# A gated MLP with ternary down projection on one core: down_w's loads and roundings, the first batch's order, and VectorE's planned work in slots 7 and 8

## The chip, the core and the metric

The kernel runs on one core of a Trainium2 chip. The time is the device time of one execution in microseconds (us); runs of the kernel before gave 723.7, 724.06 and 725.07, so its median is 724.06. One more execution was profiled. The engines of the core work on their own instruction queues: PE (TensorE, matrix products), DVE (VectorE), ACT (ScalarE), POOL (GpSimd), and SP (SyncE), which here only issues DMA transfers. Each engine takes its instructions in program order, and an instruction that waits holds back all behind it on its engine.

## What is computed

```python
scale = cond @ norm_w.T + 1.0
ms = jnp.mean(x * x, axis=-1, keepdims=True)
h = x * (scale[:, None, :] * jax.lax.rsqrt(ms + EPS))
u = h @ up_w.T
val, gate = jnp.split(u, 2, axis=-1)
h = val * jax.nn.gelu(gate, approximate=False)
y = act_quant(h) @ weight_quant(down_w).T        # forward value
return y + x
```

`act_quant` scales each token by 127 over its largest magnitude, rounds, clips and scales back; `weight_quant` makes down_w ternary (-1, 0, 1) with one scale, the mean of its magnitudes. x is 4 x 1024 x 512, up_w 4096 x 512 (2048 rows of value, 2048 of gate), down_w 512 x 2048, all in float32.

## The kernel before, in words

**Batches and slots.** The four batches of x are worked off one after the other, each in 16 slots. A slot makes 128 of the 2048 hidden features for the batch's 1024 tokens (two halves of 512). Precision comes from splitting each float32 operand into a high and a low float16 part (`s_high`, `s_low` and their likes make them, in ACT and in DVE or POOL).

**The product.** From slot 13 of batch 1 on, a slot is a Strassen-like form with 7 products, each of six matmuls (class `Slot`, `product` at L690), on sums of weight blocks and sums of token blocks. The products go to PSUM banks A, E and B: `first` (A), which ACT copies to B (`first_copy`, L797), `fourth` (E), `second` (on to B), `third` (A), `fifth` (A), `gate` (E) and `value` (A). DVE and ACT close the slot: `third_out` (L825) and `value_out` (L845) on DVE write the hidden activations H, `gate_sum` (L833) on DVE frees the E bank, and two Gelus run on ACT. Slots 0 to 12 of batch 1 are done without it: each half has a gate and a value of 12 matmuls (`half_gate`, `half_gelu`, `half_value`, `half_out`, L705 to L761), because the sums of weights are not there yet.

**The weights.** In batch 1 each slot's weight rows are loaded (`w_load`), scaled by a power of two (`w_range`, `w_factor`, `w_scale`), split (`w_rows_high`, `w_rows_low`), turned by a transposing DMA (`w_rows_turn`), and then summed for the 7-product form: `s_sum` (L429) makes four sums of a slot in float32, `s_high` (L446) and `s_low` (L450) split them. Both `s_sum` and `s_low` run on POOL, or on DVE where the step's name ends in a further `.1`. For slots 13 to 15 the split sums stand in rows (`s_rows`, two buffers of the tag `xr`) and are turned by `s_turn` (L468). All sums are stored in HBM by `s_spill` (L462), and each later batch loads them back, slot by slot, two slots ahead: `s_load` (L478, L476) with four parts named `s_load.g.n`, where slot g counts on from 16 for batch 2. They go to the double buffer SXY.

**down_w.** Its eight parts of 512 KB are fetched a second time by `d_fetch(n)` (L539), rounded by `d_round` (L543) and made ternary by `d_sign` (L550), both on ACT, the latter into a buffer of the tag `xr`, and turned pairwise by `d_turn` (L553) into `wd`. The buffers of the fetches are borrowed from the tokens. Parts 0 to 5 are fetched in the first batch; `D_MOVES` has the fetches and turns that follow in slots of batch 2, and `D_LATE` the roundings and signs, with their slot and their place in it (x, y or z).

**Down projection.** That of a batch runs in slots 10 to 13 of the next one, which makes those slots longer (15.2 us against 9.07).

**What sets the order.** For the first batch an order written out by hand: the string `FIRST_BATCH` (L1355) holds 609 steps such as `s_low.15.0` (name, slot, part) and `slot.15.1` (slot, index in `SLOT_STEPS`: 0 `first`, 1 `first_copy`, 2 `fourth`, 7 `second_gelu`, 11 `gate_sum` and so on), and `take` (L1350) issues them one by one. This gives the program order of every engine, SP included. It ends with the transfers for slots 0 and 1 of batch 2 (`s_load.16.n`, `s_load.17.n`). `t_turn.3` (L665), the turn of the last tokens of batch 2, stands among the steps before them.

For batches 2 to 4 a planner (`Filler`, L1441) places the rest of DVE's and ACT's work, above all the largest magnitude of each token (`pair_max`, L886 to L898). Each item has a cost in us and a slot from which it may run. Each slot has a budget:

```python
left = SLOT_US + PAIR_US * down - OWN_US + 0.4
more = D_SUM_US * len(late_sums) + 0.7 * (j + 1 == min(DOWN) and b + 1 < B)
left -= D_SUM_US * len(early_sums) + more
```

(L1574 to L1576; SLOT_US is 9.07). `run(p)` (L1581) then spends it at the places x and z of the slot, and what does not fit waits for the next one.

Of the kernel before, what the change touches and what calls it, by code (L numbers as in the profile page):

```python
# [51 lines left out]
def glu_quant_kernel(  # L52
# [1297 lines left out]
    def take(steps):  # L1350
# [5 lines left out]
        w_load.3 d_load.6 d_load.3 t_load.0 d_load.5 d_load.4 s_sum.0.1 o_whole.2.2.0 gate.1.0 w_range.3  # L1356
        x_scale.6 w_factor.3 gelu.1.0 turn.4 s_sum.0.0.1 turn.5 w_load.4 x_scale.7 s_sum.0.2 w_range.2
        turn.6 turn.7 w_load.5 o_whole.0.0.0 x_high.0 value.1.0 x_high.3 x_low.0 d_load.2 d_load.7 x_high.1
        x_low.3 x_high.2 w_factor.2 s_high.0.0 x_low.1 d_sum.4 x_low.2 gate.0.1 o_whole.1.0.1 out.1.0
        w_scale.2.1 w_scale.2.0 value.0.1 s_sum.0.3.1 rows_high.2 s_high.0.1 rows_low.2 rows_turn.2  # L1360
        w_scale.3.1 w_scale.3.0 o_WHOLE.3.2.1 gelu.0.1 gate.1.1 rows_high.3 s_low.0.0.1 d_sum.5 w_load.9
        s_sum.1.0.1 s_sum.1.2.1 w_range.4 rows_low.3 value.1.1 s_low.0.1.1 s_spill.0.0 gelu.1.1 s_sum.1.3.1
        t_square.0.0 out.1.1 d_load.0 s_high.1.1 gate.2.0 w_range.5 c_largest w_factor.4 d_sum.6 s_sum.1.1.1
        w_load.10 o_sum.0 s_high.1.0 rows_turn.3 value.2.0 out.0.1 w_scale.4.1 d_sum.7 s_low.1.0 w_scale.4.0
        c_over w_factor.5 gate.2.1 s_sum.2.0 rows_high.4 o_sum.1 w_scale.5.0 s_low.1.1 s_spill.1.0 c_range
# [5 lines left out]
        c_spread s_spill.2.2 c_rows gate.4.0 out.3.0 t_square.0.1 w_scale.6.1 s_sum.3.2 max.0.0.0 d_sum.1
        s_sum.3.3 max.1.0.0 o_high.0 s_sum.3.1 w_load.8 value.4.0 t_root.0 w_scale.6.0 max.1.0.1 rows_high.6
        out.3.1 s_high.3.0 o_low.0 gate.4.1 w_range.7 rows_low.6 rows_turn.6 gelu.4.0 w_factor.7 s_high.3.1
        w_scale.7.1 s_low.3.1.1 value.4.1 s_low.3.0.1 s_sum.4.1 w_scale.7.0 gelu.4.1 s_sum.4.0 s_spill.3.0
        c_undo rows_high.7 t_load.1 c_copy d_total out.4.0 gate.5.0 w_range.8 rows_low.7 rows_turn.7 out.4.1
        s_sum.4.2.1 s_sum.4.3 value.5.0 s_high.4.0 w_factor.8 c_store w_gain.6 s_low.4.0.1 w_scale.8.1
        s_spill.5.1 s_spill.6.1 gelu.5.0 s_sum.5.0.1 c_load s_sum.5.1 out.5.0 w_scale.8.0 d_spread gate.5.1
        rows_high.8 max.0.1.0 rows_low.8 value.5.1 rows_turn.8 gelu.5.1 s_sum.5.2.1 w_range.9 s_high.4.1
        s_low.4.1 w_factor.9 gate.6.0 max.1.1.0 w_scale.9.0 s_sum.5.3 s_high.5.0 d_mean gelu.6.0 max.1.1.1
        s_spill.3.2 s_low.5.0.1 s_spill.4.0 value.6.0 s_spill.7.1 c_bring w_scale.9.1 s_spill.5.0 out.5.1  # L1380
        w_gain.8 t_scale.0.1 s_high.5.1 s_low.5.1 rows_high.9 s_sum.6.0.1 gate.6.1 s_spill.8.1 s_sum.6.1.1
        t_scale.0.0 s_sum.6.2.1 t_high.0.0 rows_low.9 s_high.6.0 value.6.1 rows_turn.9 t_high.0.1
        t_sum.0.0.1 w_range.10 t_low.0.0 t_sum.0.1.1 t_sum.0.2.1 gelu.6.1 w_factor.10 w_scale.10.1
        t_sum.0.3.1 gate.7.0 s_low.6.0.1 t_high.0.2 out.6.0 s_sum.7.0 w_scale.10.0 s_sum.6.3.1 s_spill.4.2
        t_low.0.2 s_high.6.1 s_spill.5.2 value.7.0 rows_high.10 s_low.6.1.1 w_gain.10 t_low.0.1 t_turn.0
        t_square.1.1 out.6.1 t_square.1.0 s_sum.7.1.1 s_sum.7.2.1 gate.7.1 t_root.1 s_sum.7.3.1 w_range.11
        t_scale.1.1 s_high.7.0 w_factor.11 w_scale.11.0 s_low.7.0.1 value.7.1 gelu.7.0 s_spill.6.0
        rows_low.10 rows_turn.10 s_high.7.1 s_low.7.1 gelu.7.1 out.7.0 w_scale.11.1 gate.8.0 s_sum.8.0.1
        s_sum.8.1.1 s_sum.8.2.1 s_high.8.0 out.7.1 s_spill.7.0 s_sum.8.3.1 s_high.8.1 value.8.0 s_low.8.0.1
        s_spill.8.0 gelu.8.0 s_sum.9.0.1 s_low.8.1.1 s_spill.8.2 s_sum.9.1.1 s_sum.9.2.1 s_high.9.0  # L1390
        s_low.9.0 t_scale.1.0 gate.8.1 s_sum.9.3.1 w_load.12 rows_high.11 max.2.0.0 s_spill.6.2 w_range.12
        rows_low.11 value.8.1 rows_turn.11 max.2.0.1 t_sum.1.0.1 out.8.0 t_sum.1.2 max.3.0.0 gate.9.0
        gelu.8.1 t_sum.1.3 max.3.0.1 w_factor.12 w_scale.12.0 s_spill.9.1 out.8.1 t_load.2 value.9.0
        s_spill.11.1 t_high.1.1 t_sum.1.1.1 s_high.9.1 s_low.9.1 s_sum.10.1.1 gelu.9.0 max.2.1.0 t_high.1.2
        s_sum.10.0 max.2.1.1 w_scale.12.1 gate.9.1 s_sum.10.2 max.3.1.0 s_spill.9.2 rows_high.12 s_spill.7.2
        s_spill.9.0 s_sum.10.3.1 s_high.10.1 max.3.1.1 w_load.13 value.9.1 rows_low.12 rows_turn.12
        t_low.1.2 out.9.0 s_high.10.0 gate.10.0 gelu.9.1 t_high.1.0 t_square.2.1 t_low.1.0 w_range.13
        t_low.1.1 t_turn.1 value.10.0 out.9.1 s_low.10.0.1 gelu.10.0 t_square.2.0 s_low.10.1.1 s_sum.11.0.1
        t_root.2 s_sum.11.2.1 gate.10.1 w_factor.13 s_sum.11.3 s_sum.11.1.1 s_high.11.1 t_scale.2.1
        w_load.14 s_high.11.0 t_load.3 t_scale.2.0 value.10.1 w_scale.13.0 t_sum.2.0.1 w_scale.13.1 out.10.0  # L1400
        rows_high.13 s_low.11.0.1 s_spill.11.0 w_range.14 s_sum.12.0.1 gate.11.0 s_sum.12.1.1 s_spill.10.1
        s_sum.12.2.1 s_spill.10.2 s_low.11.1.1 s_spill.12.1 t_sum.2.2.1 t_sum.2.1.1 s_spill.10.0 rows_low.13
        rows_turn.13 s_high.12.0 value.11.0 t_sum.2.3.1 t_high.2.1 w_factor.14 w_gain.12 t_high.2.2
        s_low.12.0.1 t_low.2.2 t_high.2.0 gelu.10.1 gate.11.1 out.10.1 gelu.11.1 s_spill.12.0 t_low.2.1
        t_low.2.0 t_turn.2 s_sum.13.1.1 value.11.1 s_sum.12.3.1 s_sum.13.0.1 s_sum.13.2.1 gelu.11.0 out.11.1
        s_high.12.1 t_square.3.0 s_high.13.0 gate.12.0 t_square.3.1 w_scale.14.0 s_low.13.0.1 s_sum.14.0
        out.11.0 w_load.15 s_turn.13.0 value.12.0 s_low.12.1.1 gelu.12.0 t_root.3 s_sum.13.3.1 s_spill.13.0
        s_high.13.1 w_scale.14.1 s_low.13.1.1 rows_high.14 s_sum.14.2 s_turn.13.1 gate.12.1 out.12.0
        s_sum.14.3 s_spill.13.2 w_range.15 rows_low.14 rows_turn.14 t_scale.3.1 value.12.1 s_high.14.0
        s_low.14.0 s_sum.14.1.1 t_sum.3.0.1 w_factor.15 w_scale.15.0 s_turn.14.0 w_scale.15.1 slot.13.0  # L1410
# [404 lines left out]
```

## Time and profile before

| what | value |
|---|---|
| median of the runs | 724.06 us (723.7 to 725.07) |
| the profiled execution | 723.61 us, of which the span of the trace is 721.8 us |
| PE | busy 714.7 us, 99% of the span |
| DVE | 589.7 us, 82% |
| ACT | 422.0 us, 58% |
| POOL | 126.0 us, 17% |
| mean granted clock of PE | 0.999 |
| HBM | 53.50 MB read, 23.09 MB written |

The trace has a start and a duration for every instruction. A row of a timeline reads: start in us from the span's beginning, duration, engine, line of the kernel, operation, output <- inputs, and in square brackets how long the engine stood idle before and what it waited for. PEld is the loading of weights into the array, which runs beside the products; SPq are the DMA issues on SP's queue. A chain of waits goes back from the end of the program, at each step to what released the work; "issue" is time in which an engine waited for nothing that the trace shows.

### The profile page before, as it was taken

How to read it: one execution, taken by the hardware profiler on the slowest of the kernel's cores; microseconds unless marked ns; L12 is line 12 of the kernel's file. 1: busy time of each engine (PE TensorE's matmuls, PEld its weight loads, DVE VectorE, ACT ScalarE, POOL GpSimd, SP SyncE). 2: the span in 40 equal slices, each digit the busy share in tenths (PEclk: the TensorE clock that was granted, in tenths of full speed). 3: DMA queues.
4: the chain of work that ended last, by engine and by line, in shares of the span. 5: the costliest groups of instructions: out<-in, count | busy, mean ns of one | idle time of the engine just before them, and what ended most of it. 6: DMA issues, size and time to landing. Idle time of an engine off the chain costs nothing.

```text
span 721.8 us, 10211 instructions
## 1 busy us (share of the span) xinstructions
PE 714.7 (99%) x3670; PEld 360.1 (50%) x3670; DVE 589.7 (82%) x889; ACT 422.0 (58%) x700; POOL 126.0 (17%) x132
## 2 busy tenths in 40 slices
PE   8999999999999999999999999999999999999998
PEld 4544444444444446665444445665444444445854
DVE  8898998877898899887789887676688888755896
ACT  6998875776667774554335676544433665333473
POOL 1532222140100124340100030460020000000120
PEclk9999999999999999999999999999999999999999
DMA  7799987999995665777845646765944545442253
GB/s 277 259 280 288 245 200 231 281 219 258 278 189 117 132 160 146 192 185 165 172 102 101 129 101 188 178 166 162 212 103 103 102 102 103 101 102 90 103 175 117
DMA packets 230003, 123.01 MB, mean 170 GB/s; under 512 B 191401, under 2 KB 201277, under 8 KB 229954
## 3 DMA queue, kind: packets, MB, share of 16 engines
q1 hardware_dynamic: 229802, 122.24, 68.3%
q8 instruction: 28, 0.46, 0.3%
q14 instruction: 21, 0.17, 0.1%
q10 hardware_dynamic: 152, 0.13, 0.1%
HBM read 53.50 MB, written 23.09 MB: 106 GB/s over the span
## 4 chain that ended last, share of the span: by engine, by line
PE 95%; DMA 1%; ACT 1%; DVE 1%; SPq 1%; issue 1%; DVEq 0%; ACTq 0%
PE A L690 35%; PE E L690 17%; PE po L1052 9%; PE pg L705 9%; PE pv L705 9%; PE B L690 9%; PE po_end L1004 4%; DMA SXY<-s_dram 1%; PE pz L1169 1%; DMA s_dram<-s_rows 1%; PE ptx L1153 1%; PE pv L776 0%; PE po_B L1052 0%; PE pg L776 0%; PE pw L375 0%
## 5 line engine op out<-in xcount | busy, mean ns | idle before, releaser
L690 PEld LDWEIGHTS <-SXY 128*128 128x128 f16 x2100 | 205.4, 98 | 242.2 <-issue 1.3
L690 PE MATMUL A<-R,SXY 128*128 128x512 f16 x1164 | 269.0, 379 | 0.5 <-DMA SXY<-s_dram 0.5
L690 PE MATMUL E<-R,SXY 128*128 128x512 f16 x588 | 142.9, 379 | 0.1
L825 DVE SCALAR_TENSOR_TENSOR H<-A,sg,t 128x512 f32<-128x512 f32 x51 | 38.3, 750 | 71.0 <-PE A L690 70.9
L976 DVE TENSOR_TENSOR H<-H,am 128x1024 f32<-128x1024 f32 x64 | 76.1, 1215 | 0.0
L836 ACT ACTIVATE t<-t,sg 128x512 f32<-128x512 f32 x51 | 36.8, 721 | 65.7 <-DVE t L833 65.6
L690 PE MATMUL B<-R,SXY 128*128 128x512 f16 x300 | 72.9, 379 | 0.3 <-ACT B L797 0.3
L896 DVE TENSOR_REDUCE gm<-H 128x512 f32<-128x1024 f32 x56 | 69.0, 1232 | 1.1
L705 PEld LDWEIGHTS <-SXY 128*128 128x128 f16 x390 | 38.1, 98 | 45.9 <-DVE SXY L417 0.4
L819 ACT ACTIVATE t<-B,sg 128x512 f32<-128x512 f32 x51 | 35.0, 687 | 35.6 <-PE B L690 35.5
L912 POOL PARTITION_ALL_REDUCE am<-R x8 | 14.3, 1793 | 233.2 <-DVE R L898 233.2
L1052 PE MATMUL po<-wd,R 128*128 128x256 fp8e4 x416 | 52.4, 273 | 0.0
L812 ACT COPY t<-A 128x512 f32<-128x512 f32 x51 | 29.6, 580 | 36.1 <-PE A L690 35.8
L805 ACT COPY v<-E 128x512 f32<-128x512 f32 x51 | 29.9, 585 | 32.3 <-PE E L690 27.3
L1052 PEld LDWEIGHTS <-R 128*128 128x128 bf16 (+1 forms) x448 | 43.8, 98 | 8.9
L705 PE MATMUL pg<-R,SXY 128*128 128x512 f16 x204 | 46.8, 379 | 0.0
L797 ACT COPY B<-A 128x512 f32<-128x512 f32 x51 | 29.2, 572 | 29.9 <-PE A L690 29.2
L845 DVE SCALAR_TENSOR_TENSOR H<-v,sg,t 128x512 f32<-128x512 f32 x51 | 40.1, 786 | 6.4 <-ACT t L836 6.3
L705 PE MATMUL pv<-R,SXY 128*128 128x512 f16 x186 | 43.4, 379 | 0.0
L984 ACT ACTIVATE H<-H 128x1024 f32<-128x1024 f32 x38 | 39.9, 1050 | 5.2 <-DVE H L976 5.2
L842 DVE TENSOR_TENSOR v<-A,v 128x512 f32<-128x512 f32 x51 | 34.9, 684 | 8.8 <-PE A L690 7.6
L898 DVE TENSOR_TENSOR R<-R,gm 128x512 f32<-128x512 f32 x56 | 40.9, 730 | 1.1
(236 smaller groups left out, 926.2 us busy)
## 6 DMA issues: line engine op xcount, KB each, us to landing
SXY<-s_dram SPq DMA_DIRECT2D x48, 256.0 KB, 2.9
H<-in_L_cond_up_w_dram SPq DMA_DIRECT2D x13, 512.0 KB, 4.1
s_dram<-SXY SPq DMA_DIRECT2D x16, 384.0 KB, 3.6
SXY<-s_dram SPq DMA_DIRECT2D x48, 128.0 KB, 3.1
xr<-in_x_dram SPq DMA_DIRECT2D x19, 256.0 KB, 3.1
out_dram<-xr SPq DMA_DIRECT2D x19, 256.0 KB, 2.5
H<-in_x_dram SPq DMA_DIRECT2D x8, 512.0 KB, 7.7
R<-in_L_cond_down_w_dram SPq DMA_DIRECT2D x8, 512.0 KB, 6.9
```

What stands on the lines that cost most here:

```text
L690: PE.matmul(o, s[:, w, k, :], operand(g // NJ, c, l, k), start=start and n == 0, stop=stop and n == len(TERMS) - 1, skip_group_check=True,)
L705: PE.matmul(ps, a[k // 2][:, w, k % 2, :], XP[:, l, k, h * TOK : (h + 1) * TOK], start=n == 0, stop=n == len(terms) - 1,)
L819: ACT.activation(self.t1, self.B, AF.Gelu, scale=gain(self.g, 1))
L825: DVE.scalar_tensor_tensor(h_half(self.g, 0), self.A, gain(self.g, 0), self.t1, ALU.mult, ALU.mult)
L836: ACT.activation(self.t2, self.t2, AF.Gelu, scale=gain(self.g, 1))
L842: DVE.tensor_tensor(self.v, self.A, self.v, ALU.add)
L845: DVE.scalar_tensor_tensor(h_half(self.g, 1), self.v, gain(self.g, 0), self.t2, ALU.mult, ALU.mult)
L896: DVE.tensor_reduce(gm[0], v, AX.X, ALU.max, apply_absolute_value=True)
L898: return [largest, lambda: DVE.tensor_tensor(m, m, gm[0], ALU.max)]
L976: DVE.tensor_tensor(v, v, r.to_broadcast([P, 2, TOK]), ALU.mult)
L984: ACT.activation(v, v, AF.Copy, bias=MAGIC)
L1052: PE.matmul(po, w[:, j], m, start=start and j == 0, stop=stop and j == n - 1, skip_group_check=True,)
```

## The change

It has three parts. (1) `KEPT_US` takes 3.0 us off the planner's budget in slots 7 and 8, in every batch but the last. (2) The fetches of down_w's parts 4 and 5 leave the first batch for slots 0 and 1 of batch 2, the turns 2 and 3 of down_w stand in slots 3 and 4, and parts 4 to 7 are rounded and signed a slot later. (3) `FIRST_BATCH` is written in a new order. PE's instructions stay in the old order. 14 steps of sums and differences go from POOL to DVE (among them `s_sum.2.0`, `s_sum.14.0`, `s_sum.15.1`, `s_sum.15.3`, `t_sum.3.2`) and 14 from DVE to POOL (among them `s_sum.0.0`, `s_low.12.1`, `s_sum.15.0`, `t_sum.3.1`, `s_low.15.0`); SP has two steps less. Of the string only the lines around slot 4 and the end are shown.

```diff
     D_LATE = [
         ((0, "x"), d_round, 2), ((0, "x"), d_sign, 2), ((0, "y"), d_round, 3),
-        ((1, "x"), d_sign, 3), ((1, "x"), d_round, 4), ((1, "y"), d_sign, 4),
-        ((2, "x"), d_round, 5), ((2, "x"), d_sign, 5), ((2, "y"), d_round, 6),
-        ((3, "x"), d_sign, 6), ((3, "x"), d_round, 7), ((3, "y"), d_sign, 7),
+        ((1, "x"), d_sign, 3), ((2, "x"), d_round, 4), ((2, "x"), d_sign, 4),
+        ((2, "y"), d_round, 5), ((3, "x"), d_sign, 5), ((3, "x"), d_round, 6),
+        ((3, "y"), d_sign, 6), ((4, "x"), d_round, 7), ((4, "x"), d_sign, 7),
     ]
     D_MOVES = {
-        0: ((d_turn, 0),),
-        1: ((d_turn, 1), (d_fetch, 6)),
-        2: ((d_turn, 2), (d_fetch, 7)),
+        0: ((d_turn, 0), (d_fetch, 4)),
+        1: ((d_turn, 1), (d_fetch, 5), (d_fetch, 6)),
+        2: ((d_fetch, 7),),
+        3: ((d_turn, 2),),
         4: ((d_turn, 3),),
     }
...
     FIRST_BATCH = """
...
-        rows_turn.4 o_high.3 s_sum.2.2.1 gate.3.0 s_sum.2.3.1 out.2.0 s_high.2.1 rows_high.5 s_low.2.1
-        o_sum.2 d_sum.2 value.3.0 w_gain.4 o_sum.3 d_sum.3 o_high.2 o_low.1 w_load.6 gelu.2.1 rows_low.5
...
+        gate.3.0 s_sum.2.0.1 rows_high.5 s_sum.2.2.1 s_sum.2.3.1 o_low.1 o_high.2 s_high.2.1 rows_low.5
+        value.3.0 d_sum.2 s_spill.2.1 w_load.6 o_sum.3 w_load.11 d_sum.3 w_gain.4 s_low.2.1.1 gelu.2.1
...
-        rows_turn.15 t_high.3.0 slot.13.6 gains s_low.14.1.1 slot.13.5 t_high.3.2 t_low.3.0 slot.13.13
-        s_sum.15.1 gelu.12.1 s_turn.14.1 s_sum.15.3 s_high.15.0 slot.14.0 out.12.1 t_high.3.1 slot.13.3
-        s_spill.14.2 t_low.3.2 d_fetch.1 slot.13.7 slot.14.2 slot.14.1 slot.13.14 s_high.15.1 s_low.15.1
-        s_spill.13.1 t_low.3.1 slot.14.6 s_low.15.0.1 s_turn.15.0 slot.13.8 s_spill.15.0 d_round.0 t_turn.3
-        slot.14.4 slot.13.9 max.4.0.0 slot.13.10 slot.14.5 slot.14.3 max.4.0.1 slot.14.13 slot.13.11
-        max.5.0.0 slot.13.12 slot.15.0 d_sign.0 s_turn.15.1 slot.13.15 max.5.0.1 slot.14.7 slot.15.2
-        s_load.16.0 slot.15.1 s_spill.15.1 max.4.1.0 s_load.16.1 d_round.1 slot.15.6 slot.14.14 slot.15.3
-        max.4.1.1 d_fetch.2 slot.14.8 slot.15.7 s_spill.15.2 max.5.1.0 slot.15.4 slot.15.5 slot.14.9
-        slot.14.10 d_sign.1 slot.15.13 s_load.17.1 slot.14.11 slot.15.14 slot.14.12 max.5.1.1 max.6.0.0
-        d_fetch.3 s_spill.11.2 s_load.16.3 slot.14.15 max.6.0.1 s_load.17.0 s_load.16.2 max.6.1.0
-        s_spill.12.2 d_fetch.5 max.6.1.1 s_spill.14.1 d_fetch.4
...
+        t_sum.3.1 t_sum.3.2.1 slot.13.4 t_high.3.0 s_spill.13.1 gelu.12.1 out.12.1 s_spill.14.0 slot.13.6
+        slot.13.5 t_high.3.1 t_sum.3.3.1 slot.13.3 t_low.3.0 slot.13.13 t_high.3.2 rows_low.15 rows_turn.15
+        slot.13.7 t_low.3.2 slot.14.0 slot.14.1 t_low.3.1 slot.14.2 slot.13.14 s_spill.14.2 gains
+        s_sum.15.2.1 s_high.15.0 s_low.15.0 d_fetch.1 max.4.0.0 slot.14.6 s_turn.15.0 w_gain.15 slot.13.8
+        slot.13.9 slot.14.7 slot.14.4 s_spill.15.0 s_sum.15.3.1 s_high.15.1 s_low.15.1 t_turn.3 slot.13.10
+        slot.14.5 slot.14.3 slot.14.13 d_round.0 slot.13.11 max.4.0.1 d_sign.0 slot.15.0 max.5.0.0 slot.15.1
+        slot.15.2 s_turn.15.1 max.5.0.1 d_round.1 slot.14.14 s_load.16.0 slot.15.6 max.4.1.0 s_load.16.1
+        d_sign.1 slot.14.8 max.4.1.1 slot.13.12 d_fetch.2 max.5.1.0 s_spill.15.1 d_fetch.3 slot.15.4
+        s_spill.15.2 slot.13.15 slot.14.9 slot.14.10 slot.15.5 slot.15.3 slot.15.7 slot.15.13 slot.14.11
+        slot.15.14 slot.14.12 slot.14.15 max.5.1.1 s_load.17.0 max.6.0.0 s_spill.14.1 s_load.17.1 max.6.0.1
+        s_spill.12.2 max.6.1.0 s_load.16.3 max.6.1.1 s_spill.11.2 s_load.16.2
     """
...
     OWN_US = 3.0
+    KEPT_US = {7: 3.0, 8: 3.0}
...
             left -= D_SUM_US * len(early_sums) + more
+            if b + 1 < B:
+                left -= KEPT_US.get(j, 0)
```

More of the change, by code (lines that the diff above doesn't have):

```diff
@@ L1355, in glu_quant_kernel @@
     FIRST_BATCH = """
[L1356 to L1365, printed above, removed]
@@ L1371, in glu_quant_kernel @@
[L1371 to L1380, printed above, removed]
@@ L1381, in glu_quant_kernel @@
[L1381 to L1410, printed above, removed]
@@ new lines, in glu_quant_kernel @@
+        out.2.1 gate.3.1 s_high.2.0 gelu.3.0 o_low.3 w_load.7 d_sum.0 o_low.2 value.3.1 w_range.6
+        s_spill.3.1 s_spill.4.1 s_low.2.0.1 s_sum.3.0 rows_turn.5 gelu.3.1 w_factor.6 t_square.0.1 out.3.0
+        c_spread w_scale.6.0 c_rows gate.4.0 s_spill.2.2 s_sum.3.1 max.0.0.0 w_scale.6.1 s_spill.2.0 d_sum.1
+        s_sum.3.2.1 max.1.0.0 s_sum.3.3 rows_high.6 t_root.0 value.4.0 o_high.0 rows_low.6 rows_turn.6
+        w_range.7 out.3.1 o_low.0 gate.4.1 s_high.3.0 w_factor.7 w_load.8 t_load.1 gelu.4.0 s_low.3.0.1
@@ new lines, in glu_quant_kernel @@
+        t_sum.0.2.1 w_factor.10 w_scale.10.1 t_sum.0.3 s_low.6.0.1 s_sum.7.0 gate.7.0 w_gain.10 t_high.0.2
+        out.6.0 s_sum.6.3.1 w_scale.10.0 t_low.0.2 s_high.6.1 rows_high.10 value.7.0 out.6.1 t_square.1.0
+        s_low.6.1.1 t_low.0.1 t_turn.0 t_square.1.1 s_sum.7.1.1 s_sum.7.2.1 t_root.1 t_scale.1.1 gate.7.1
+        w_range.11 s_sum.7.3.1 s_high.7.0 w_factor.11 gelu.7.0 s_low.7.0.1 value.7.1 s_high.7.1 gelu.7.1
+        rows_low.10 s_spill.7.0 w_scale.11.0 s_spill.5.2 out.7.0 s_spill.6.0 s_spill.6.2 s_low.7.1.1
@@ new lines, in glu_quant_kernel @@
+        gate.8.0 rows_turn.10 s_sum.8.0.1 s_sum.8.1.1 s_sum.8.2.1 s_high.8.0 out.7.1 s_sum.8.3.1
+        w_scale.11.1 s_low.8.0.1 s_spill.8.0 s_high.8.1 value.8.0 gelu.8.0 s_sum.9.0.1 s_low.8.1.1
+        rows_high.11 s_sum.9.1.1 s_sum.9.2.1 s_high.9.0 s_low.9.0 t_scale.1.0 s_sum.9.3.1 w_load.12 gate.8.1
+        w_range.12 max.2.0.0 t_load.2 rows_low.11 value.8.1 rows_turn.11 max.2.0.1 t_sum.1.0.1 out.8.0
+        t_sum.1.2 max.3.0.0 gelu.8.1 gate.9.0 t_sum.1.3 t_high.1.1 max.3.0.1 w_factor.12 w_scale.12.0
@@ new lines, in glu_quant_kernel @@
+        t_sum.1.1.1 s_spill.8.2 out.8.1 s_high.9.1 s_low.9.1 s_spill.9.1 value.9.0 t_high.1.2 max.2.1.0
+        s_spill.11.1 s_sum.10.1 w_scale.12.1 max.2.1.1 rows_high.12 s_sum.10.0.1 max.3.1.0 gate.9.1
+        s_sum.10.2 t_high.1.0 s_spill.7.2 s_spill.9.0 s_sum.10.3.1 t_low.1.2 w_load.13 s_spill.9.2
+        rows_low.12 value.9.1 rows_turn.12 gelu.9.1 gelu.9.0 max.3.1.1 t_square.2.1 out.9.0 s_high.10.0
+        t_low.1.1 gate.10.0 gelu.10.0 out.9.1 t_low.1.0 s_low.10.0.1 t_turn.1 s_sum.11.0.1 value.10.0
@@ new lines, in glu_quant_kernel @@
+        s_sum.11.2.1 t_square.2.0 s_high.10.1 s_low.10.1.1 t_root.2 w_range.13 gate.10.1 t_scale.2.1
+        s_sum.11.3 w_factor.13 s_sum.11.1 s_high.11.0 w_load.14 t_sum.2.0.1 out.10.0 t_load.3 value.10.1
+        w_scale.13.0 t_scale.2.0 s_high.11.1 t_sum.2.1.1 w_scale.13.1 t_sum.2.2.1 gelu.10.1 s_low.11.0.1
+        s_spill.11.0 rows_high.13 gate.11.0 s_low.11.1.1 t_sum.2.3.1 w_range.14 s_spill.10.1 s_sum.12.0.1
+        s_spill.12.1 s_sum.12.1.1 s_sum.12.2.1 s_spill.10.0 s_high.12.0 rows_low.13 value.11.0 t_high.2.2
@@ new lines, in glu_quant_kernel @@
+        w_factor.14 s_low.12.0.1 s_spill.12.0 w_scale.14.0 t_low.2.2 t_high.2.0 rows_turn.13 w_scale.14.1
+        gate.11.1 out.10.1 t_high.2.1 t_square.3.1 s_sum.13.0.1 t_square.3.0 t_low.2.0 t_low.2.1 t_turn.2
+        w_gain.12 t_root.3 gelu.11.1 value.11.1 out.11.1 s_sum.12.3 gelu.11.0 s_sum.13.1 s_high.12.1
+        rows_high.14 s_sum.13.2 s_low.12.1 s_high.13.0 gate.12.0 gelu.12.0 s_sum.13.3.1 t_scale.3.1
+        w_load.15 out.11.0 s_low.13.0.1 s_turn.13.0 value.12.0 t_sum.3.0.1 s_high.13.1 s_sum.14.0.1
@@ new lines, in glu_quant_kernel @@
+        rows_low.14 s_spill.13.0 s_low.13.1.1 s_turn.13.1 w_range.15 gate.12.1 w_gain.14 w_factor.15
+        s_spill.10.2 s_sum.14.1.1 w_scale.15.1 s_spill.13.2 w_scale.15.0 value.12.1 t_scale.3.0 rows_turn.14
+        out.12.0 d_fetch.0 slot.13.0 s_sum.14.2.1 s_high.14.0 s_low.14.0 s_sum.14.3.1 s_high.14.1
+        s_low.14.1.1 s_turn.14.0 s_sum.15.0 s_sum.15.1.1 slot.13.2 slot.13.1 s_turn.14.1 rows_high.15
+        t_sum.3.1 t_sum.3.2.1 slot.13.4 t_high.3.0 s_spill.13.1 gelu.12.1 out.12.1 s_spill.14.0 slot.13.6
```

26 lines of the change are left out of this document (21 added, 5 removed).

## The prediction

> **What bounds the kernel.** I read the page first: its span, the line of PE, and the shares of the chain that ended last.
>
> ```profile
> span 721.8 us, 10211 instructions
> PE 714.7 (99%) x3670; PEld 360.1 (50%) x3670; DVE 589.7 (82%) x889; ACT 422.0 (58%) x700; POOL 126.0 (17%) x132
> PE 95%; DMA 1%; ACT 1%; DVE 1%; SPq 1%; issue 1%; DVEq 0%; ACTq 0%
> ```
>
> PE is busy 99% of the span and 95% of the chain is PE. The diff leaves PE's instructions and their order alone. What it can win is therefore time in which PE stood still, and what it can lose is new standing still. So the second view is the busy time by windows of 20 us (the first number after the width is PE's).
>
> ```profile
> 160.00:180.00 20.00, 19.66 (x92) 8.80 (x90) 14.94 (x21) 12.35 (x19) 1.54 (x2) 1.00 1.04 252
> 180.00:200.00 20.00, 19.50 (x91) 8.73 (x90) 17.22 (x23) 13.04 (x18) 3.59 (x2) 1.00 1.09 275
> 260.00:280.00 20.00, 19.96 (x109) 10.47 (x108) 19.17 (x24) 12.54 (x21) 1.80 (x2) 1.00 0.60 159
> ```
>
> Two windows around the end of the first batch, the seam, lose 0.34 and 0.50; around 262 PE loses 0.04, and once more around 432. The granted clock is 1.00 in all of them. The timeline of PE shows the seam's two waits with their releasers, and the chain shows the other two.
>
> ```profile
> 170.04 1.46 PE L690 MATMUL E<-wd,SXY 128*128 128x512 f16 x6
> 171.83 1.45 PE L690 MATMUL B<-R,SXY 128*128 128x512 f16 x6 [0.34 <-ACT B L797]
> ...
> 188.03 1.47 PE L690 MATMUL A<-R,SXY 128*128 128x512 f16 x6 [0.50 <-DMA SXY<-s_dram]
> ```
>
> ```profile
> 259.43 2.59 PE A L690 x12
> 262.02 0.04 issue
> 262.06 1.46 PE E L690 x6
> ```
>
> ```profile
> 431.71 0.04 issue
> 431.74 1.46 PE E L690 x6
> ```
>
> Twelve matmuls take 2.59 in the chain, so a product of six starts 1.30 us after the one before it. The one at 171.83 came 1.79 after 170.04: 0.49 lost. That is 0.15 more than the idle time in its bracket, because the chain counts 1.46 for the first six after a wait, 0.16 over 1.30. In the same way the one at 188.03 lost 0.50 + 0.16 = 0.66, and those at 262.02 and 431.71 lost 0.04 + 0.16 = 0.20 each. The four sum to 1.55 us.
>
> **The ceiling.** The profiled execution took 723.61 (1.81 outside the span); the median shown is 724.06, 0.45 higher. Without the four waits it is 722.06, or 722.5 on the median's footing: 0.22%. A measurement of this kernel tells about 0.2% from no change, which is 1.45 us. Even a change that does all it can is barely visible. There is no such ceiling on a loss.
>
> **Part 1: VectorE queues less in slots 7 and 8 (KEPT_US).** At 262 the fourth product of slot 9 needs the E bank that `gate_sum` of slot 8 (L833) frees. The timeline of DVE:
>
> ```profile
> 247.81 0.75 DVE L825 SCALAR_TENSOR_TENSOR H<-A,sg,t 128x512 f32<-128x512 f32 x1 [1.31 <-PE A L690]
> ...
> 254.37 1.21 DVE L898 TENSOR_TENSOR R<-R,gm 128x512 f32<-128x512 f32 x1
> 255.62 1.25 DVE L896 TENSOR_REDUCE gm<-H 128x512 f32<-128x1024 f32 x1
> 256.90 0.69 DVE L898 TENSOR_TENSOR R<-R,gm 128x512 f32<-128x512 f32 x1
> 257.51 0.74 DVE L825 SCALAR_TENSOR_TENSOR H<-A,sg,t 128x512 f32<-128x512 f32 x1
> ...
> 261.32 0.68 DVE L833 TENSOR_TENSOR t<-E,t 128x512 f32<-128x512 f32 x1
> ```
>
> `gate_sum` ends at 262.00 and PE starts at 262.06. Between 254.37 and 257.51 DVE worked off three steps of the planned maxima, and `third_out` (257.51) queued behind them. One slot earlier it started as soon as PE released it, and a slot is seven products, 9.07 us: 247.81 + 9.07 = 256.88, so it was 0.63 late, and the three steps behind it kept that delay up to `gate_sum`. Worked through the planner, 3.0 us less in slot 7 takes all three steps of its z place out (3.15 us, 254.37 to 257.51) and one of the three in its x place. `gate_sum` then ends near 261.4, and PE needs it 0.20 before 262.06, near 261.8: the wait goes with 0.4 to spare. The same items lie in the same slots of batch 3 at 431. **−0.20 and −0.20.**
>
> What is put off must fit later. The planner moves some 3.9 us of batch 2's maxima to the end of slot 12, executed as slot 13 begins. Slots 12 and 13 of batch 2 are these windows (third number: DVE):
>
> ```profile
> 300.50:315.70 15.20, 15.20 (x100) 9.58 (x98) 14.96 (x20) 6.90 (x14) 9.04 (x11) 1.00 0.67 159
> 315.70:330.90 15.20, 15.20 (x100) 9.60 (x98) 12.03 (x18) 6.19 (x11) 3.18 (x4) 1.00 0.60 162
> ```
>
> Slot 13 would have 12.03 + 3.9 = 15.9 in 15.2, so 0.7 runs over into slot 14, but slot 12 ran at 14.96 and PE lost nothing in it. I take 0; if the overrun falls on the next `gate_sum`, it costs at most that 0.7.
>
> **Part 2: two loads and four roundings of down_w.** Two loads of 512 KB leave the seam's queue, one for each of the first two slots of batch 2. The windows above give DMA shares of 1.04 and 1.09 there: it is full, so leaving it helps whatever stands behind. The transfers of 155 to 195 have the row
>
> ```profile
> dn<-in_L_cond_down_w_dram SPq DMA_DIRECT2D x5, 512.0 KB, 5.5
> ```
>
> (median us from issue to landing). Parts 4 and 5 are rounded in slot 2, at least a slot of 9.07 after their new issue, so 5.5 is covered; a load that came later than that would hold ACT's queue by the difference. The roundings (ACT) come a slot later; ACT had 12.35 and 13.04 of 20, so I take 0, and up to 0.2 against it, the size of one slot-9 wait.
>
> **Part 3: the order of the first batch.** At the seam the chain of waits leads to two transfers:
>
> ```profile
> 164.43 4.92 DMA s_dram<-s_rows
> ...
> 182.63 5.35 DMA SXY<-s_dram
> ```
>
> and SP, which issues the transfers in order, has
>
> ```profile
> 162.92 1.45 SPq L468 DMA_TRANSPOSE SXY<-s_rows  x1
> 165.80 5.24 SPq L665 DMA_TRANSPOSE R<-nx  x1
> ...
> 182.63 1.95 SPq L478 DMA_DIRECT2D SXY<-s_dram  x2
> ```
>
> *The wait at 188* is `s_load.17.0`, landing 5.35 after its issue at 182.63, behind `s_load.17.1`, `d_fetch.3`, `s_spill.11.2` and `s_load.16.3`. In the new order it stands ahead of `s_load.17.1`, `s_load.16.3` and `s_spill.11.2`. It still has to wait until `s_spill.15.1` has landed. I put its issue at 181.5 to 182 and, since the rest of the queue is shorter, its landing at 185 to 187, against a need at 187.3. **−0.66**; if it lands no earlier, 0.
>
> *The wait at 171.8* is the copy of slot 15's first product (L797), two steps behind `d_sign.0` (L550), which waits until `s_spill.15.0` has landed and its buffer is free (164.43 + 4.92). That pair stays, and the landing decides. Two changes push it. `s_low.15.0` goes from DVE to POOL:
>
> ```profile
> L450 DVE TENSOR_TENSOR s_rows<-H,s_rows x4: 683/684/693, 143.8 to 162.2; 128x512 f16<-128x512 f32 x4
> L450 POOL TENSOR_TENSOR s_rows<-H,s_rows x2: 1159/1440/1720, 151.6 to 164.9; 128x512 f16<-128x512 f32 x2
> ```
>
> so 0.48 to 1.04 more; and `s_high.15.0`, which feeds it, now stands behind a copy of slot 14 on ACT and behind the landing of `s_spill.14.0`. Together I estimate 0.9 to 2.7 us for `s_turn.15.0` (162.92) and all that SP has behind it. For it: `d_sign.0` no longer has the Gelu of slot 14 between itself and the copy (0.67), and one load less competes. So the wait lies between gone (−0.49) and 1.4 (+0.9); I take **0**, the row as it stands.
>
> *Elsewhere in the batch* 14 sums and differences go from POOL to DVE and 14 the other way, so the load of neither changes much; I added up the work ahead of each step in the old and the new order, and it shifts by less than 1 us. The tightest place that I found is the E bank of slot 4's value, on DVE and on PE:
>
> ```profile
> 61.40 0.73 DVE L761 SCALAR_TENSOR_TENSOR H<-g,sg,pv 128x512 f32<-128x512 f32 x1
> ```
>
> ```profile
> 62.41 1.46 PE L705 MATMUL pv<-R,SXY 128*128 128x512 f16 x6
> ```
>
> The bank is free at 62.13, 0.28 ahead of its use, and the step's weights (`w_load.6`) now stand behind one more spill (`s_spill.2.1`, 128 KB). I estimate the shift at 0.2 to 0.5, which makes 0 to 0.2. With a second such place I take **0**, and up to +0.5.
>
> One rule speaks against this part. The Trainium skill, "SBUF — State Buffer", section "Who interferes with whom", says that a VectorE instruction with two SBUF inputs and a GpSimd instruction that reads SBUF exclude each other for a whole instruction. The trace agrees: in the two rows below a VectorE operation on two columns ends at 43.43, just as the GpSimd one does at 43.42. By that rule `s_low.15.0` would take the upper 1.72 whenever DVE holds such an operation, which belongs to rival B.
>
> ```profile
> 42.07 1.36 DVE L325 TENSOR_TENSOR undo<-wam,undo 128x2 int32<-128x2 int32 x1
> 41.77 1.65 POOL L450 TENSOR_TENSOR SXY<-H,SXY 128x768 f16<-128x768 f32 x1 [10.91 <-ACT SXY L446]
> ```
>
> **The sum.** −0.40 (slot 9, twice) − 0.66 (188) + 0 (171.8) + 0 (the rest) = −1.06. From 723.61 that is 722.55 for a profiled execution, and **723.0** on the median's footing: −0.15%, within what is told from no change.
>
> **The rivals.**
> A. *All four waits go.* The landing of `s_spill.15.0` comes by 169.4 and nothing else appears: −1.55, 722.5. For it: the Gelu taken out ahead of the copy and the freed queue. Against it: everything ahead of that spill comes later.
> B. *SP is late at the seam: slower.* `s_low.15.0` on POOL holds `s_turn.15.0`, and behind that `t_turn.3` (5.24 on SP), the spill and all loads of slots 16 and 17. At 2.7 late the wait at 171.8 is 1.4 (+0.9); `s_load.17.0` wins some 1.7 of issue time by its new place and loses 2.7, so the wait at 188 is 0.66 + 1.0. With −0.40 for slot 9: 723.61 + 0.9 + 1.0 − 0.40 = 725.1, on the median's footing 725.5 or 725.6. It is visible as slower from about 3.0 us of waits at the seam (1.15 now, 0.40 won back, 1.45 for the bound), which is about 2.7 us of delay. Against it: the transpose has room. Its kind lands in 4.4 by the row below, so 162.92 + 1.45 + 4.4 = 168.8 against the fourth product of slot 15 at 170.04, and a delay under 1.2 costs nothing there.
>
> ```profile
> SXY<-s_rows SPq DMA_TRANSPOSE x2, 4.4
> ```
>
> C. *The seam stays as it is*, or one wait is traded for another of its size: −0.40 alone, 723.66.
>
> **Chances and range.** Forecast 0.36, A 0.22, B 0.28, C 0.14. A, at 0.22%, counts as faster; B as slower; the others as the same: 0.22, 0.50, 0.28. The lower end is A less 0.36, by which the fastest run shown (723.7) lies below its median: 722.2 rounded up. The upper end takes in B's price, 725.5; beyond it I leave some 0.15 of B's chance. The likeliest case's own range, with the unknowns of part 3, is 722.5 to 723.9.
>
> **What would show it.** After the change PE's windows of 260 and 420 should read 20.00; if 19.96 is still there, the planner's step failed. The product that starts at 188.03 should follow without idle time, and `s_load.17.0` should be issued before 182.63. The timeline of SP should show `s_turn.15.0` between 163.8 and 165.6; earlier than that, A, and later, B. New waits at other lines in PE's list of waits, above all below 160 us or around 331, would make the prediction wrong.

## The result and the profile after

Over 22 runs each, the median went from 724.41 to 722.98 us: a ratio of 0.998 with a 95% interval of 0.9973 to 0.9988, or 0.9 to 2.0 us less. The interval does not reach 1: the gain is small, but clear of the scatter. The forecast was 723.0 against 724.06. The profiled execution after the change took 722.53 (span 720.7), that of before 723.61.

The page of the changed kernel, its span, the line of PE and the shares of the chain:

```profile
span 720.7 us, 10220 instructions
PE 714.1 (99%) x3670; PEld 359.9 (50%) x3670; DVE 591.9 (82%) x889; ACT 422.1 (59%) x700; POOL 123.0 (17%) x132
PE 95%; DMA 2%; DVE 1%; ACT 1%; issue 0%; DVEq 0%
```

The share of PE is the same, so it says nothing; the windows do (the first number after the width is PE's).

```profile
160.00:180.00 20.00, 20.00 (x95) 9.00 (x94) 15.32 (x23) 12.24 (x19) 2.69 (x3) 1.00 1.04 234
180.00:200.00 20.00, 19.55 (x90) 8.49 (x89) 17.25 (x24) 11.01 (x15) 3.59 (x2) 1.00 0.93 240
200.00:220.00 20.00, 19.57 (x92) 8.71 (x91) 17.38 (x21) 13.40 (x18) 0.00 (x0) 1.00 1.08 212
260.00:280.00 20.00, 20.00 (x111) 10.59 (x109) 18.72 (x24) 13.33 (x24) 1.94 (x2) 1.00 0.59 159
420.00:440.00 20.00, 20.00 (x95) 9.02 (x93) 13.11 (x18) 15.16 (x22) 5.51 (x6) 1.00 0.56 145
```

The losses at 171.8, 262 and 432 are gone. At 180 to 200 there is still one of 0.45, and a new one of 0.43 at 200 to 220. PE's timeline of the changed kernel shows that these are other waits than before:

```profile
183.65 1.46 PE L690 MATMUL E<-R,SXY 128*128 128x512 f16 x6
185.16 2.75 PE L690 MATMUL A<-R,SXY 128*128 128x512 f16 x12
188.24 1.47 PE L690 MATMUL E<-R,SXY 128*128 128x512 f16 x6 [0.33 <-DVE H L845]
...
194.73 2.75 PE L690 MATMUL A<-R,SXY 128*128 128x512 f16 x12
197.54 1.47 PE L690 MATMUL E<-R,SXY 128*128 128x512 f16 x6
...
204.03 2.75 PE L690 MATMUL A<-R,SXY 128*128 128x512 f16 x12
207.21 1.47 PE L690 MATMUL E<-R,SXY 128*128 128x512 f16 x6 [0.43 <-DMA SXY<-s_dram]
```

A group of six should follow after 1.30, one of twelve after 2.59. So 185.16 is 0.21 late, 188.24 is 0.49 late, 197.54 is 0.22 late and 207.21 is 0.59 late: 1.5 us in all, where the seam cost 1.15 before. From here on the size of a wait is counted in this way, as time lost, unless it is called idle time or stands in a row's bracket. The one at 185.16 waits for a copy on ACT, which stands behind a ternary step of down_w that waits for a spill:

```profile
183.49 1.15 ACT L550 ACTIVATE tn<-H,unmagic 128x1024 fp8e4<-128x1024 f32 x1 [0.45 <-DMA s_dram<-s_rows]
184.54 0.57 ACT L812 COPY t<-A 128x512 f32<-128x512 f32 x1
```

The last three are the fourth products of slots 17, 18 and 19, whose weights come by DMA. The row at 188.24 names DVE's `value_out` (L845), but that step does not touch the E bank; `gate_sum` of slot 15, which frees it, had ended at 186.66. The weight loads beside it name the true releaser:

```profile
PEld L690 <- DMA SXY<-s_dram: 2.3, 3, 0.9
```

Three waits, 2.3 us of idle time on PEld. A row of PE can name an engine that only happened to finish last; the rows of PEld read nothing but the weights.

**The two profiles, product by product.** All 3670 matmuls can be compared by their starts. From before to after the difference changes at these places only: −0.64 in the first 8 us, −0.49 at 171, +0.22 at 185, −0.66 at 188 (first product of slot 17), +0.48 at 188 (its fourth), +0.24 at 197, +0.60 at 207, −0.19 at 262, −0.20 at 432, and −0.44 behind the last product. They sum to the 1.1 us between the spans. The start scatters in both orders (`h2_spill_first`, below, has the new order and the long start of the kernel before). Without it and the end, PE's own waits balance to 0.0. So the two profiles alone do not explain what 44 runs measured, and the experiments had to.

### The profile page after: what moved, and what is told of

The parts are those of the page before. It is cut to its first block, busy times and chain, and to the rows that moved or that the text cites. A ratio compares the mean times of both kernels' runs of the same rounds, so it can differ in the third digit from the quotient of the medians.

```text
span 720.7 us, 10220 instructions
## 1 busy us (share of the span) xinstructions
PE 714.1 (99%) x3670; PEld 359.9 (50%) x3670; DVE 591.9 (82%) x889; ACT 422.1 (59%) x700; POOL 123.0 (17%) x132
## 4 chain that ended last, share of the span: by engine, by line
PE 95%; DMA 2%; DVE 1%; ACT 1%; issue 0%; DVEq 0%
PE A L690 34%; PE E L690 18%; PE po L1052 9%; PE pg L705 9%; PE pv L705 9%; PE B L690 9%; PE po_end L1004 4%; DMA SXY<-s_dram 2%; PE pz L1169 1%; PE ptx L1153 1%; DVE gm L896 1%; PE pv L776 0%; PE po_B L1052 0%; PE pg L776 0%; DVE R L898 0%; PE pw L375 0%
## 5 line engine op out<-in xcount | busy, mean ns | idle before, releaser
L845 DVE SCALAR_TENSOR_TENSOR H<-v,sg,t 128x512 f32<-128x512 f32 x51 | 40.1, 786 | 6.6 <-ACT t L836 6.5
```

Of the source, the lines that this page charges most:

```text
L845: DVE.scalar_tensor_tensor(h_half(self.g, 1), self.v, gain(self.g, 0), self.t2, ALU.mult, ALU.mult)
```

## The experiments

**The parts one by one, and the kernel before once more.** `e1_kept` is the kernel before with

```diff
+    KEPT_US = {7: 3.0, 8: 3.0}
...
+            if b + 1 < B:
+                left -= KEPT_US.get(j, 0)
```

> The kernel before with KEPT_US alone. Theory 1 (each part acts where it stands): the two waits of slot 9's fourth product, 0.19 and 0.20 us in the trace, go, and nothing else on PE changes: the seam keeps its waits of 0.49 and 0.66, the time falls by 0.4 us (ratio 0.9995). Rival (what is put off comes back): DVE is late in slot 13 or 14 of batch 2 or 3, a new wait of 0.2 to 0.7 us stands on PE near 331 or 500, and the time is the same or longer.

723.65 against 723.96, ratio 1.0 (0.999 to 1.001): too small for the timing, but not for the trace. In PE's timeline of `e1_kept` no group is late around 262:

```profile
259.13 2.75 PE L690 MATMUL A<-R,SXY 128*128 128x512 f16 x12
261.72 1.46 PE L690 MATMUL E<-R,SXY 128*128 128x512 f16 x6
```

2.59 later, as it should be; the one at 432 went too, and nothing came near 331 or 500. Theory 1 holds for this part. The seam stayed, but not with its size:

```profile
171.21 1.46 PE L690 MATMUL B<-R,SXY 128*128 128x512 f16 x6 [0.58 <-ACT B L797]
187.90 1.47 PE L690 MATMUL A<-R,SXY 128*128 128x512 f16 x6 [0.99 <-DMA SXY<-s_dram]
```

They stand 0.58 and 0.99 idle where the first profile had 0.34 and 0.50, with the same order of the same steps.

`e2_moves` is the kernel before with the new `D_LATE` and `D_MOVES`, and `d_fetch.4` and `d_fetch.5` taken from the end of `FIRST_BATCH`.

> The kernel before with the loads, turns and roundings of down_w alone (two loads out of the first batch into slots 0 and 1 of batch 2, four parts rounded a slot later). Theory 1: the waits at 171.8 and 188.0 stay (0.49 and 0.66), since the two loads stood behind the late one in SP's order; the loads now stand ahead of the weights of slots 18 and 19, whose fourth products wait 0.24 and 0.60 us as in the changed kernel: the time rises by 0.8 us (ratio 1.001). Rival (those two waits belong to the new order, whose last transfers come 1.3 us later on SP): no wait at 197 and 207, time the same or up to 0.6 us shorter.

724.51 against 723.96, ratio 1.0006 (0.9995 to 1.0016). The waits at 171.8 and 188 stayed, as theory 1 said. None came at 197 and 207, so there the rival is right: the moved loads alone do not make them.

`e3_order` is the kernel before with the new string, and at its end

```diff
-        s_spill.12.2 max.6.1.0 s_load.16.3 max.6.1.1 s_spill.11.2 s_load.16.2
+        s_spill.12.2 max.6.1.0 s_load.16.3 max.6.1.1 s_spill.11.2 s_load.16.2 d_fetch.5 d_fetch.4
```

> The kernel before with the new order of the first batch alone; the two loads of down_w stand at its end, as far back as they can. Theory 1: the wait at 171.8 (0.49) goes, that at 188.0 is traded for about 0.5 at the same slot, no wait at 197 and 207: time 0.5 to 0.7 us shorter (ratio 0.9992). Rival (waits at 197 and 207 belong to the order): both waits here too, 0.2 and 0.6 us or more, the time the same as before or longer.

724.36 against 723.96, ratio 1.0006 (0.9995 to 1.0017). Both waits of the seam went, as theory 1 said, but the time did not fall, and a wait that nobody had named took their place. PE and ACT in `e3_order`:

```profile
195.71 2.75 PE L690 MATMUL A<-R,SXY 128*128 128x512 f16 x12 [1.34 <-ACT t L812]
```

```profile
194.04 1.15 ACT L543 ACTIVATE dn<-dn,wsc 128x1024 f32<-128x1024 f32 x1 [1.73 <-DMA dn<-in_L_cond_down_w_dram]
195.09 0.57 ACT L812 COPY t<-A 128x512 f32<-128x512 f32 x1
```

ACT waits 1.73 for down_w's part 4, which now stands at the end of a longer queue; the copy of slot 17's fifth product stands behind it, and PE stands idle 1.34 for the copy. In the complete change that rounding comes a slot later. Neither the order nor the moves alone made the kernel faster, and this one trace says why the order needs the later rounding. How large the wait is in other executions is not shown: the profiled one, 723.08, was the fastest of the twelve.

`e0_before`, unchanged:

> The kernel before, unchanged, for a second profile. If the waits of PE are fixed by the program, the four waits come again within 0.1 us each, and only the start (up to 8 us) and the end differ between profiles; if the seam's waits vary from execution to execution, those at 171.8 and 188.0 differ by several tenths.

One run, 723.99. The two waits of slot 9 were the same to 0.01 us; those of the seam were 0.24 and 0.60. And a fifth wait stood there, in the first batch:

```profile
49.63 1.68 PE L705 MATMUL pg<-R,SXY 128*128 128x512 f16 x7 [1.22 <-DMA SXY<-H]
```

It comes in some executions of the old order and not in others: 0 (before), 1.39 (`e0_before`), 0 (`e1_kept`) and 0.95 us (`e2_moves`), and 0.78 in `h4_pool6`, below. In all eight profiles of the new order it is absent. What it waits for is the turn of slot 3's weights. SP in the kernel before (no wait), in `e0_before` (wait) and in the changed kernel:

```profile
42.32 3.66 SPq L399 DMA_TRANSPOSE SXY<-H  x1
```

```profile
39.69 0.38 SPq L299 DMA_DIRECT2D H<-in_L_cond_up_w_dram  x1
41.79 5.64 SPq L399 DMA_TRANSPOSE SXY<-H  x1
```

```profile
39.08 3.48 SPq L399 DMA_TRANSPOSE SXY<-H  x1
42.62 0.57 SPq L299 DMA_DIRECT2D H<-in_L_cond_up_w_dram  x1
```

In the old order two weight loads, `w_load.9` and `w_load.10`, go ahead of the turn; the row at 39.69 is the second. Where no wait came, the turn's issue ended at 46.0 or before; where one came, at 47.1 to 47.4 (three profiles), for a product due between 48.0 and 49.0. In the new order only `w_load.10` goes ahead and `w_load.9` is the row at 42.62, behind the turn, whose issue ends at 42.6.

`f4_turn3` tried to show this by one step of the kernel before: `rows_turn.3` right after `rows_low.3`, and `w_load.9` behind it.

> The kernel before with one step moved in the first batch: slot 3's weights are turned right after they are split, ahead of two weight loads, as in the new order. Theory 1 (the old order has a wait near 49 us that comes in some executions, 0.95 and 1.39 us in two of four profiles, none in the others): no wait near 49 in the profile, and the median falls by about 0.6 us (ratio 0.9992), none of it at the seam. Rival (the wait is only a mark of a disturbed start): a wait there as before, or the time no shorter.

726.35 against 724.01, ratio 1.0037 (1.0023 to 1.0051): slower. In this kernel the turned weights overwrite slot 0's sums before they are stored, so later batches use other numbers for slot 0; and two other waits came, 1.4 and 0.8 of idle time, on DVE's `out` at 41.7 and on a Gelu at 50.6. The one on the DMA near 49 did not. The step was moved too far, ahead of both weight loads where the new order passes only one, to separate theory and rival, so the cause of the wait at 49 is read from SP's rows and not isolated by a run.

**The new waits.** `f1_fetch_last` is the changed kernel with

```diff
-                        g + 2, [lambda f=f, n=n: f(n) for f, n in moves]
+                        g + 2, [lambda f=f, n=n: f(n) for f, n in moves if f is d_turn]
...
                     s_load_y(g + 1)
+                for f, n in D_MOVES.get(j, ()) if b == 1 else ():
+                    if f is d_fetch:
+                        f(n)
```

> The changed kernel with down_w's loads in batch 2 issued behind both weight loads of their slot, not between them. Theory 1 (the waits at 197 and 207 are the moved loads, standing ahead of the weights of slots 18 and 19): both waits, 0.24 and 0.60 us, go, and those at 185.2 (0.22) and 188.2 (0.48) stay. Rival (they come from the queue that the new order leaves behind at the seam): both stay within 0.2 us.

One run, 724.03. The waits at 197 and 207 went, but so did those at 185 and 188, which the edit does not touch; and larger ones came, 1.7 on PE at 209.2 and 0.5 at 217.5. The first is there because ACT now waits for the load of part 5:

```profile
206.92 1.15 ACT L543 ACTIVATE dn<-dn,wsc 128x1024 f32<-128x1024 f32 x1 [3.54 <-DMA dn<-in_L_cond_down_w_dram]
```

So the loads do not stand too early in the changed kernel: they have no room to come later.

`f2_spill_sign` is the changed kernel with

```diff
-        d_sign.1 slot.14.8 max.4.1.1 slot.13.12 d_fetch.2 max.5.1.0 s_spill.15.1 d_fetch.3 slot.15.4
+        d_sign.1 slot.14.8 max.4.1.1 slot.13.12 s_spill.15.1 d_fetch.2 max.5.1.0 d_fetch.3 slot.15.4
...
-        ((0, "x"), d_round, 2), ((0, "x"), d_sign, 2), ((0, "y"), d_round, 3),
+        ((0, "x"), d_round, 2), ((0, "y"), d_sign, 2), ((1, "x"), d_round, 3),
```

> The changed kernel with the spill of slot 15's second part issued ahead of the load of down_w's part 2, and part 2 made ternary one place later (behind the copy of the fifth product). Theory 1: the waits at 185.2 (0.22: that copy behind the ternary step, which waits for a spill) and 188.2 (0.48: slot 17's weights, which cannot be loaded before that spill has landed) go; those at 197 and 207 stay. Rival (the queue is full, so the order on SP only changes who waits): the sum of the waits between 180 and 210 stays within 0.3 us of 1.54.

One run, 721.53, and a profile with 0.1 us of waits between 180 and 210, those at 197 and 207 gone too, which neither theory 1 nor the rival had said. What the swap does can be read in SP's queue; the first row is `s_load.17.0` in the changed kernel, the second in `f2_spill_sign`:

```profile
181.51 0.33 SPq L478 DMA_DIRECT2D SXY<-s_dram  x1
```

```profile
177.72 0.33 SPq L478 DMA_DIRECT2D SXY<-s_dram  x1
```

It overwrites what slot 15's spill still reads, so it waits for that spill to land, and SP waits with it from 176.3 to 181.5 in the changed kernel, holding all loads behind. The swap did not bring this transfer itself in earlier: it landed 3.5 after its issue in the changed kernel and 7.6 after in `f2_spill_sign`, at 185.1 and 185.4. What came earlier is the one behind it, `s_load.17.1`, again first in the changed kernel and then in `f2_spill_sign`:

```profile
182.41 2.81 SPq L476 DMA_TRANSPOSE SXY<-s_dram  x1
```

```profile
178.78 3.76 SPq L476 DMA_TRANSPOSE SXY<-s_dram  x1
```

`g_all` has both edits, `h1_spill_sign` is `f2_spill_sign` again, timed, and `h2_spill_first` has only the swap of the spill.

> The changed kernel with both edits, loads of down_w behind the weights and the spill of slot 15 ahead of part 2 with its ternary step a place later. Theory 1: all four waits between 180 and 210 go, 1.5 us, and the time is 2.5 to 3 us below the kernel before (ratio 0.9960 to 0.9965), some 1.4 below the changed one. Rival (the queue is full and the waits move on): waits of about the same sum at other slots up to 220, and the time as that of the changed kernel (ratio 0.998).

> The changed kernel with the spill of slot 15's second part ahead of the load of part 2, and part 2 made ternary one place later, timed in rounds. One profile of this kernel had no wait left between 180 and 210. If that holds from execution to execution, the median is 1.3 to 1.5 us below the changed kernel's and 2.5 to 3 below the kernel before (ratio 0.996 to 0.9965), and this profile again has under 0.3 us of waits there. Rival (that profile was a lucky one): waits at 188, 197 or 207 again, the ratio 0.998.

> The changed kernel with only the spill of slot 15's second part ahead of the load of part 2. If the late spill is what delays slot 17's weights and, through SP's queue, those of slots 18 and 19, the waits at 188, 197 and 207 go (1.3 us) and that at 185.2 (0.2) stays. Rival (the later ternary step does it): the waits at 197 and 207 stay.

`g_all`: 722.99 against 724.01, ratio 0.9985 (0.9975 to 0.9996). The four waits went and 1.7 us came at 208 to 217, as in `f1_fetch_last`. `h1_spill_sign`: 721.79 against 723.97, ratio 0.9966 (0.9954 to 0.9979), but its second profile has 1.1 us of waits there again:

```profile
188.27 1.47 PE L690 MATMUL E<-R,SXY 128*128 128x512 f16 x6 [0.47 <-DMA SXY<-s_dram]
...
191.21 2.76 PE L690 MATMUL A<-R,SXY 128*128 128x512 f16 x12 [0.17 <-DMA SXY<-s_dram]
```

The waits are as the rival had them, so the first profile was a lucky one; the time is as theory 1 had it. The profiled execution, 722.19, is the second slowest of its six, so most of the others may have had less of them. `h2_spill_first`, one run of 722.17, has 0.5 of waits: those at 185 and 188 went, those at 197 and 207 stayed, 0.2 and 0.3. That is the sign of its rival, but with 0.1 and 1.1 in two profiles of one kernel a single profile does not decide it. `h1_spill_sign` is the fastest version timed here. That it beats the kernel before is shown; that it beats the changed one is likely, since its interval only just overlaps that one's.

**The wait at 171.8.** `h3_spill13` is the changed kernel with `s_spill.13.1` moved from its place ahead of `gelu.12.1` to right before `s_turn.15.0`.

> The changed kernel with one spill of 384 KB (slot 13's second part) moved back to its old place on SP, right ahead of the turn of slot 15's first sums. Theory: the wait at 171.8 went because this spill left the queue ahead of slot 15's spill; here that spill lands 1 us or more later after its issue than in the changed kernel, the ternary step of part 0 waits, and a wait of 0.2 to 0.7 us is back on PE near 171. Rival (it went because the Gelu of slot 14 left ACT's queue ahead of the copy): no wait near 171.

One run, 721.84. The spill ahead did matter: in ACT's rows of `h3_spill13` the ternary step waits 0.40, where no wait stands in the changed kernel.

```profile
168.91 1.15 ACT L550 ACTIVATE tn<-dn,unmagic 128x1024 fp8e4<-128x1024 f32 x1 [0.40 <-DMA s_dram<-s_rows]
169.96 0.58 ACT L797 COPY B<-A 128x512 f32<-128x512 f32 x1
```

But PE did not wait, because the copy follows at once: it ends at 170.54, and PE's product starts at 170.96, on time. My theory fell. In the old order a Gelu of 0.67 stood between these two rows; with it the copy would have ended near 171.2, too late. So the rival holds by these rows, though no run put the Gelu back alone. Between 180 and 210 this kernel has 0.6 of waits, the changed one 1.5, and the two profiles of `f2_spill_sign`, one kernel, 0.1 and 1.1: the seam's new waits scatter as the old ones did.

**The end of the program.** Behind the last product the kernel before takes 0.44 us longer than the changed one. The last issue is that of the output:

```profile
span 721.8 us, 10211 instructions
718.82 0.38 ACTq L1014 DMA_DIRECT2D out_dram<-R  x1
q14 instruction: 21, 0.17, 0.1%
```

```profile
718.18 0.38 ACTq L1014 DMA_DIRECT2D out_dram<-R  x1
q14 instruction: 22, 0.18, 0.1%
```

From that issue to the end of the span it is 3.0 in the first fence, of before, and 2.5 in the second, with the span of 720.7 above. In the trace of before, GpSimd stands still for 0.32 us between two of its very last instructions (721.09 to 721.41), and after the change for 0.03. The new order has 205 GpSimd instructions where the old one has 199: 132 of work in both, and six more waits and the like on its queue. The instruction behind the pause takes 0.18 where it takes 0.04 after the change, which with the pause makes the 0.44. `h4_pool6` gives the kernel before six more:

```diff
+    idle = cpool.tile([P, 1], F32, name="idle")
+    for _ in range(6):
+        POOL.memset(idle, 0.0)
```

> The kernel before with six tiny GpSimd instructions more, in the last batch. In the kernel before the end of the program, behind the last product, takes 3.56 us, in every kernel with the new order 3.12; in the former GpSimd stands still for 0.32 us between its last two instructions. Theory: the new order gives GpSimd six instructions more (205 against 199), which moves a fixed pause of its instruction stream to an earlier place where it costs nothing; here the end takes 3.1 us. Rival (it comes from the order of the work itself): 3.56 us as before.

One run, 724.4, with the wait of 0.8 near 49. Its end took 3.12 behind the last product, and the page has

```profile
q14 instruction: 22, 0.18, 0.1%
```

The theory holds: the 0.44 hangs on the count of GpSimd's instructions, and six idle ones do what the new order does. The traces say more. In thirteen of the fourteen profiles the pause, 0.32 to 0.38, stands right ahead of GpSimd's 197th instruction, wherever that falls: at 721.1 in the kernel before, at 692.9 in the changed one, where it costs PE nothing. With one instruction more than before (200, `f4_turn3`) it stands one step of the closing sequence earlier and costs 0.14 less. With 206 (`h3_spill13`) it does not show. In each of the thirteen the last transfer of queue 14, which carries instructions, starts 0.7 to 1.0 after the pause: at 722.12 in the kernel before, behind the end of the span, and at 694.0 after the change. That is why the row counts 21 and 22; with those outside the span there are 35 in every profile, and this one only comes earlier. It starts behind the pause, so the pause is no wait for it, and what the pause is stays open.

## Why the prediction was right, and where it was not

The total agrees: 723.0 forecast, 722.98 measured, a gain of 1.06 forecast and 1.43 (0.9 to 2.0) measured; that the times agree to 0.02 is chance, since the median of before came out at 724.41 and not 724.06. The terms agree less well.

- *Slot 9, −0.40.* Right in mechanism and size: −0.39 between the profiles, alone in `e1_kept` too. `gate_sum` of slot 8 ended at 261.13, on the time scale of the profile before at 261.4, as forecast. What was put off cost nothing; slots 12 and 13 of batch 2 lost no time on PE.
- *The wait at 188, −0.66.* Right that it goes, and by the named step: `s_load.17.0` was issued at 181.51 (forecast 181.5 to 182) and PE's first product of slot 17 did not wait. Wrong as a sum: I followed the one transfer that was late and not those behind it on SP. `s_load.17.1` became the late one, then those of slots 18 and 19. I named nothing that would be late next; it was 1.5 us in the changed kernel and 0.6 in `h3_spill13`.
- *The wait at 171.8, taken as 0.* It went, −0.5. I weighed an estimated delay of 0.9 to 2.7 against the Gelu's 0.67 and let them cancel. On the time scale of the profile before, `s_turn.15.0` was indeed 1.3 later (163.62, plus the 0.64 by which this execution started earlier, against 162.92) and inside the forecast 163.8 to 165.6. But the delay had no price, since the spill behind it also had one of 384 KB less ahead of it, and the Gelu alone was enough.
- *Elsewhere in the first batch, taken as 0 (0 to +0.5).* Wrong in sign. The new order takes away the wait near 49, which is 0 to 1.4 in five profiles of the old order, 0.62 in the mean. The one profile that I had is an execution without it, so no row could show it.
- *The end.* Not in the sum at all: −0.44, by a count of instructions.
- *The ceiling of 0.22%.* Wrong for the last two reasons. It was the sum of one execution's waits, and `h1_spill_sign`, with the same products on PE, gained 0.34%. The 0.2% as the least that can be told from no change was too coarse as well: the measured interval is 0.15% wide.
- *Rival B* had a delay, 1.3 and not 2.7, and not its price: no wait at 170. By the Trainium skill ("SBUF — State Buffer", "Who interferes with whom") a reduction on VectorE never contends with GpSimd on trn2. The trace agrees for the 0.37 us in which the two ran together: GpSimd's `s_low.15.0` took 1.16 and not 1.72. An operation of DVE with two inputs in SBUF did not meet it here, so the rule that the prediction named was not tested at this step.

```profile
161.57 1.23 DVE L896 TENSOR_REDUCE gm<-H 128x512 f32<-128x1024 f32 x1
...
162.43 1.16 POOL L450 TENSOR_TENSOR s_rows<-H,s_rows 128x512 f16<-128x512 f32 x1 [6.52 <-ACT s_rows L446]
```

- *Rival C* is nearest to what the two profiles show at the seam: waits of one size traded for others.

By the mean of the profiles: slot 9 −0.40, the end −0.44, the wait at 49 −0.62, those at 171.8 and 188 −0.50 and −0.81 (five profiles of the old order), and +1.1 for the new waits (1.5 in the changed kernel and, taken as a second draw, 0.6 in `h3_spill13`) make −1.7, inside the measured interval. So the total was right by luck in good part: the gains that I left out, about 1.6, were near to a loss that I left out, 1.1. The sum is argued from few profiles, and for `e3_order` it fails: with 1.5 lost at 195.7 it gives −0.9, where +0.4 (−0.4 to +1.2) was measured. How large the seam's waits are in the other executions stays open, and so does why the wait near 49 comes in some and not in others.

## What to carry to other kernels

- A wait that hangs on a DMA is one draw: the old order gave 0.60 to 1.15 us at one product, and 0 to 1.4 at another. Before a ceiling is drawn from a profile, look at two or three. Count as certain only a wait with no DMA behind it, like that of slot 9, which came again to 0.05 us in every profile that has it; the wait at 171.8 names ACT, but a spill stands behind it, and it was 0.25 to 0.75.
- When a late transfer is moved forward in a full queue, follow the next two or three transfers to their users as well; the one to move may be the transfer whose landing the whole queue waits for, here one spill.
- A wait in an engine's queue costs what stands between it and the copy that PE needs: a wait of 0.4 us cost nothing where no Gelu stood behind it any more.

## What the runs showed of the hardware

The issue of a transposing DMA holds SP's queue for very different times, 3.48, 3.66, 4.10, 5.20 and 5.64 us for the same turn of slot 3's weights (the kernel changed, the kernel before, `e1_kept`, `e2_moves`, `e0_before`). GpSimd pauses 0.32 to 0.38 us ahead of its 197th instruction, and the end of a program takes 3.55 or 3.12 us behind the last product by where that falls (199 or 205 instructions).
